# Loading query weights from ScalarE's queue and gate/up weights as 32x32 blocks, with the order of steps made anew

## The chip, the cores and the metric

One core of one Trainium2 chip. The metric is device time of one execution of the kernel, in microseconds (us), and the number compared is the median of several runs. A core has a matrix engine (TensorE, PE in the profile; its weight loads are shown as PEld), VectorE (DVE), ScalarE (ACT), GpSimd (POOL) and SyncE (SP). SP and ACT also issue transfers (DMAs) from memory; in the profile their issues are shown as SPq and ACTq. Each engine runs its own instructions in order; between engines there are semaphores.

## What is computed

For each of 16 batch elements x (256 tokens of 256 channels): attention with 16 heads under a mask, an RMS norm with a gain and a shift made from a condition vector, a time-mixing layer with a linear recurrence, a rotation, and a gated feed-forward layer whose operands are quantized to FP4 in blocks of 16. Cut to its frame (the weights of the first layer are written Wq to Wo, those of the mixing layer ak to ao):

```python
q, k, v = x @ Wq.T, x @ Wk.T, x @ Wv.T              # 16 heads of 16
o = softmax(q @ k.T * 0.25, masked) @ v @ Wo.T
xn = rms_norm(o) * (1 + sc) + shift                  # sc, shift = silu(cond) @ Wc.T + bc
x = x + (sigmoid(r) * wkv_scan(k2, v2)) @ ao.T       # k2, v2, r: xn mixed with its neighbour, @ ak, av, ar
xq = quant(rotate(x))                                # one 256x256 rotation from cond and q_right
h = silu(xq @ quant(w_gate).T) * (xq @ quant(w_up).T)
out = x + quant(h) @ quant(w_down).T
```

w_gate and w_up are 704x256, w_down is 256x704. quant divides each block of 16 by its largest absolute value over 6, rounds to the FP4 grid and multiplies back.

## The kernel before, in words

Each batch element goes through stages, each a Python generator that yields after a few instructions: `ask` (a: load and transpose x, project q, k, v), `attend` (t), `leave` (l: output projection and norm), `mix` (m), `rotate` (r), `hidden` (h, i: gate and up for each half of the tokens), `turn_h` (d, e) and `down` (f). Beside them stand the stages that prepare the weights: `loads` (L), `turn_w` (Q for Wq, Wk, Wv; O for Wo; A for ak, av, ar, ao), `turn_mask` (K), `modulate` (M), `times` (T), `rotation` (R), `in_weights` (W0 to W5) and `out_weights` (V0, V1). The string ORDER at lines 27 to 75 names, token by token, which generator takes its next step; that is the order of the program, and each engine gets its instructions in it. Nothing reorders them later.

Transfers. `loads` (line 209) issues in this order: x of element 0 as four transfers (`load_x`, line 139, on SP: one for each group of 64 channels, in pieces of 64 floats, so that 32x32 blocks lie where VectorE's block transpose wants them), Wq, the 13 small vectors (line 222, on ACT's queue, into the tile `rows`), Wk, the mask, Wv, Wo, Wc, and the four matrices of the mixing layer. All but the vectors are issued by SP. Transfers use eight semaphores in turn: one that takes a semaphore waits until the transfer that had it before has landed, and what is behind it on its queue waits too.

Weights. `turn_w` (line 292) transposes a matrix on PE in four 128x128 pieces into a PSUM bank and copies the bank out (q, k, v, o on DVE, line 305; the others on ACT, line 307). `in_weights(j)` (line 514) loads up to two groups of 128 rows of the concatenated gate and up weights (128x256 each, 1 KB a row), quantizes them as 128x512 (the last block as 128x256), transposes them on PE (line 531) and copies them from PSUM into `guT` on ACT (line 535). There are six such blocks.

`quant` (line 481) is used for weights and activations alike: on DVE the largest absolute value (488), its scaling (490), a reciprocal (491) and a product (492); on ACT an absolute value (494); on DVE two rounding steps (496, 497); on POOL the product back (500). I call lines 488 to 492 the first half and 496 to 497 the second. Its small tiles are double-buffered. x of each element is transposed by DVE in 32x32 blocks (line 605). `turn_mask` makes `keep` from the mask, which the value copies of every element read (line 640). `modulate` makes `sil` on DVE (352 to 354), which a matmul reads (358); `rotation` writes 32 small products on POOL (423, 428) that DVE multiplies by `mgain` (433) before PE combines them (439).

PSUM: four banks serve the scores (`pss`), four everything else (`ps`), taken in turn, so that each use of a `ps` bank waits for the reader of the fourth use before it.

Before all of it stand 12 transposes of the identity into an unused bank (line 183), and POOL's memsets.

Of the kernel before, what the change touches and what calls it, by code (L numbers as in the profile page):

```python
# [17 lines left out]
P = 128  # L18
# [6 lines left out]


ORDER = """
L L L L W1 L Q Q L K L a0 W5 a0 W1 W1 K K Q Q Q W1 Q a0 L W1 a0 R a0 K a0 L W5 R L W0 W1 K K K W5 A R t0 a0 L A
W1 O t0 L a0 W3 R W5 W5 W0 M a1 A O t0 A W5 a1 R M a2 W5 t0 t0 t0 a1 R a1 t0 W0 W3 t0 R W3 W3 t0 W2 a1 t0 t0 a1
M a1 t1 a1 W0 A W3 V0 t1 t1 R R A M t0 W0 W3 a2 R t1 W0 V0 M t1 W2 t1 t0 W3 t1 t1 W4 a3 V1 W0 t0 A t0 M t0 t1 V0  # L30
t0 a3 t0 A T W2 W2 t1 T t1 V0 t1 a2 a2 a2 t1 l0 a2 t1 a2 t1 V0 l0 l0 t1 V0 a2 W4 W2 t1 l0 V0 a4 l0 l0 t2 l0 m0
t1 V1 W4 a3 t2 t2 a3 a3 m0 m0 m0 m0 m0 t2 t2 a3 W4 V1 t2 m0 m0 m0 l1 l1 l1 m0 m0 m0 l1 t2 W4 m0 m0 m0 m0 m0 t2
t2 t2 t2 l1 V0 l1 l1 a3 a3 V0 t2 t2 r0 V1 t2 W4 m1 m1 t2 W2 m1 m1 r0 a4 m1 t3 m1 W4 t3 t2 m1 m1 V1 t2 t3 t3 t2
W2 V1 r0 t3 t3 m1 m1 m1 m1 r0 V1 a4 l2 l2 m1 m1 m1 m1 t3 m1 a4 r0 t3 l2 t3 t3 a4 t3 t3 l2 r1 r1 r0 t3 r0 a4 l2
t3 t3 r1 r1 r1 l2 l2 a4 a4 a5 t3 r0 r0 a5 r0 m2 m2 t4 t4 t3 t3 m2 m2 a6 i0 i0 i0 i0 t4 i0 i0 i0 i0 i0 i0 i0 i0
i0 i0 m2 m2 m2 m2 m2 r1 r1 r1 r1 m2 t4 t4 m2 t4 r1 m2 a5 a5 a5 a5 a5 a5 m2 l3 t5 l3 t4 l3 l3 h0 m2 m2 m2 t4 t5
m2 h0 h0 h0 h0 h0 h0 l3 h0 h0 h0 r2 t5 l3 l3 V1 h0 i1 h0 r2 t4 r2 a6 V1 h0 m3 t4 i1 a7 h0 r2 i1 h1 i1 r2 t4 h1
h1 i1 t4 h1 t4 t4 h1 h1 h1 t4 m3 m3 a6 h1 h1 t5 a6 h1 r2 h1 r2 t4 t5 t4 i1 a6 r2 r2 t5 h1 h1 i1 r2 m3 a6 t5 i1
i1 i1 i1 t5 t5 h1 m3 t5 t4 t5 t5 a6 a6 m3 m3 t6 t6 m3 m3 m3 i1 i1 m3 m3 i2 i2 i2 i2 i2 m3 e0 e0 i2 i2 t6 t6 e0
i2 l4 i2 t6 i1 i2 i2 t6 h2 h2 e0 t5 m3 m3 m3 l4 h2 t6 l4 h2 m3 h2 t6 l4 h2 i2 h2 h2 h2 h2 t5 r3 h2 t5 l4 r3 a7  # L40
d0 l4 t5 h2 t6 t5 t5 l4 i2 m4 d0 d0 m4 a8 h2 t6 d0 h2 i2 a7 r3 t6 a7 a7 t6 t6 t6 t6 a7 m4 m4 m4 r3 r3 a7 a7 m4
m4 m4 t7 l5 t7 t7 l5 m4 m4 m4 m4 m4 t6 t7 l5 l5 l5 r3 m4 m4 e1 m4 m4 l5 l5 t7 t6 t6 f0 f0 f0 f0 r4 t7 r3 r4 a8
r3 e1 e1 e1 r3 f0 t7 t7 t7 d1 d1 r4 t7 t7 d1 r3 r4 i3 a9 d1 r4 i3 m5 m5 i3 i3 i3 i3 i3 a8 r4 m5 m5 i3 i3 i3 t7
a8 a8 a8 i3 i3 i3 m5 m5 t8 m5 m5 m5 l6 l6 a8 a8 l6 r4 h3 h3 l6 t8 t8 m5 h3 h3 h3 f1 m5 m5 t8 t8 i3 l6 t8 h3 f1
m5 m5 h3 h3 t7 r4 r4 r4 f1 l6 m5 m5 l6 h3 h3 h3 m5 t8 t8 t7 t7 t7 t7 t8 r5 t8 f1 t8 i4 i4 m6 t8 t8 r5 a9 d2 h3
h3 i4 d2 i4 aa i4 t8 m6 h3 t8 m6 a9 r5 r5 r5 a9 a9 a9 t8 t9 t7 d2 r5 r5 t8 t9 m6 i4 d2 r5 r5 r5 i4 i4 i4 i4 e2
m6 e2 m6 a9 i4 e2 i4 t8 e2 a9 m6 m6 l7 i4 l7 m6 m6 m6 t9 l7 l7 f2 f2 m6 m6 m6 m6 l7 l7 l7 l8 l8 t9 h4 m7 h4 l8
h4 m6 l8 m6 m7 f2 h4 f2 h4 h4 h4 h4 r6 h4 h4 l8 m7 m7 t9 t9 r6 l8 l8 h4 t9 t9 t9 r6 aa e3 f1 r6 i4 i5 h4 t9 e3
e3 e3 h4 i5 i5 i5 i5 t9 m8 r6 i5 m7 i5 i5 h4 r6 aa m7 i5 aa t9 t9 t9 ab t9 m8 i5 i5 i5 d3 f2 m7 r6 d3 h5 h5 h5
h5 h5 aa aa h5 i5 r6 r6 ta t9 h5 t9 h5 m7 h5 ta ta h5 h5 m7 h5 aa ta r6 h5 m8 aa m7 d3 d3 m7 m7 m7 m7 h5 m7 f3  # L50
m7 m7 f3 f3 f3 m8 m8 ta ta ta m8 ta m8 ta r7 r7 m8 m8 m8 ta ta d4 d4 ta i5 ta ta ta ab f3 i6 i6 i6 i6 i6 i6 i6
i6 i6 i6 i6 h6 h6 h6 h6 h6 h6 h6 h6 h6 h6 i6 ab ab ab ab d4 d4 ta tb h6 m8 h6 t9 m8 e4 e4 i6 h6 ab m8 ta ta e4
m8 ac r7 m8 l9 tb m8 i6 ab e4 f4 f4 l9 r7 h6 r7 f4 l9 l9 l9 m8 e5 tb r8 tb f4 l9 l9 f4 r8 d5 ac m9 m9 m9 r8 e5
r8 r7 r7 tb m9 la d5 r7 la la m9 m9 r8 la ac ac m9 m9 m9 m9 m9 r8 r7 tb m9 d5 m9 r7 ac m9 la d5 la la m9 ac tb
m9 tb tb i7 ma ma tb tb ad i7 i7 i7 i7 i7 i7 i7 i7 e5 e5 i7 i7 i7 tb tc tc tc m9 r8 i7 f5 f5 i7 ma f5 f5 d6 f5
r8 d6 r9 tb h7 r9 tb h7 ad r8 tb ma r8 h7 h7 h7 h7 r9 r9 h7 h7 h7 ma ma tb r9 ma r9 tc tc tc tb h7 h7 h7 ad ad
tb r9 ac ac ma ma ma ma ma h8 h8 h8 tc ma ma d6 h8 h8 d6 tc ad i8 ma ma ad r9 i8 i8 i8 i8 i8 i8 h8 h7 h8 tc i8
i8 i8 h7 ma h8 e6 h8 e6 e6 e6 h8 lb h8 h8 r9 f6 lb i8 i8 r9 f6 h8 f6 f6 ra i8 lb lb lb f6 tc tc ra e7 lb lb e7
tc h8 i8 i9 tc i9 i9 i9 ae tc ra tc mb e7 i9 mb ad ra ra td d7 e7 i9 ad tc ra i9 ae d7 td td mb mb ra tc i9 tc
i9 mb td td h9 ra i9 mb i9 mb td mb h9 mb h9 i9 h9 h9 h9 mb h9 h9 h9 d7 d7 td h9 h9 td td i9 h9 h9 lc lc td lc  # L60
af mb ae ra mb lc f7 mb mb i9 ae lc lc ra mb f7 mb lc mc ia mc h9 ia ia ia ia f7 f7 ia ia ia td ia ia ia ia mb
rb rb td td d8 td ae rb f7 ia td rb ae ae mc d8 te td mc d8 mc ae rb ia d8 rb td e8 mc td mc mc af mc e8 e8 e8
mc mc mc rb mc ld mc mc f8 te mc te te rb rb ld ld ld te ha f8 f8 ha mc ha ha rb te ha f8 ha ha ha te ha ib ha
ha ha te te te te te ib ha rc ib ib ib ib ib ib ld ld ld te rc ha ib rc ib ib e9 hb d9 rc md e9 af te rc md hb
ib hb f8 te hb md hb ib e9 md d9 af te te af e9 hb rc rc ib rc te C md af hb hb hb hb hb d9 d9 tf md af af md rc
rc hb hb le le md md tf f9 tf le md md f9 le md tf md md md md md tf tf ic ic ic ic ic f9 f9 ic ic ic le hb rd
ic le ic tf ic rd le ic me f9 rd tf ic da tf rd rd da ea hc ea hc hc rd ea ic me hc da ea tf hc rd hc tf da me
me me me tf tf hc rd me hc hc tf tf hc hc me me hc me tf tf rd tf hc me fa me me me me fa fa rd db fa me lf id
db lf fa id id id id lf lf id id id me db id id id hc lf C hd hd lf db hd lf id hd hd eb re id eb eb hd hd mf mf
id eb hd re re hd fb re hd dc hd re fb fb mf re dc fb hd mf fb mf mf re hd mf ec ec ec dc dc mf ec re fc hd mf  # L70
fc mf fc mf mf ed re fc dd fc ed mf re dd mf mf mf mf ed ie ed ie ie ie ie ie ie ie dd rf dd ie ie he C he ie he
rf rf ie C rf he ie he ie he rf fd he he he rf rf rf fd he fd he rf ee fd rf if if he he if ee if if he if if if
if hf hf if hf if if hf ee ee fd hf if hf de if hf hf hf de de de hf hf fe hf hf fe hf fe fe ef ef ef fe ef df
df df df ff ff ff ff ff
"""


# [1 line left out]
def kernel(  # L79
# [56 lines left out]
    x_sb = {}  # L136
    queue = [nc.sync]

    def load_x(b):
        if b < B:  # L140
            t = io.tile([P, S // 32, 64], F32, tag="x", name="x_sb", bufs=2)
            for a in range(4):
                queue[0].dma_start(
                    out=t[32 * a : 32 * a + 32], in_=x[b].rearrange("(q i) (a c) -> a i q c", i=32, a=4)[a]
                )
            x_sb[b] = t

    flat = lambda a: a.rearrange("p t e -> p (t e)")
# [31 lines left out]
    make_identity(nc, ident)  # L180

    warm = ps()
    for i in range(12):
        nc.tensor.transpose(warm[:, 0:P], ident, ident)


# [22 lines left out]
    def loads():  # L209
        def load_w(name, src, tag, bufs=1):  # L210
            w_in[name] = lent(tag, bufs)
            if name == "ao":

                nc.sync.dma_start(out=w_in[name], in_=src.rearrange("(p h) c -> p h c", h=2))
            else:
                nc.sync.dma_start(out=w_in[name], in_=src.rearrange("(t p) c -> p t c", p=P))

        load_x(0)
        yield
# [8 lines left out]
        yield  # L228
        load_w("k", w_k, "er")
        yield  # L230
        nc.sync.dma_start(out=mask_u, in_=mask.rearrange("(t p) k -> p t k", p=P))
        yield
        load_w("v", w_v, "kv")
        yield
        load_w("o", w_o, "num")
        yield
# [275 lines left out]
    nc.gpsimd.memset(downT[FF % P : P, FK - 1, :], 0.0)  # L512

    def in_weights(j):
        j *= 2 * P
        nt = min(2, (2 * FF - j) // P)
        n = nt * E
        raw = wk.tile([P, FF], F32, tag="h", name="raw", bufs=2)[:, 0:n]
        for jj in range(nt):
            lo, hi = j + jj * P, j + (jj + 1) * P  # L520
            for src, base in ((w_gate, 0), (w_up, FF)):
                a, b = max(lo, base), min(hi, base + FF)
                if a < b:
                    nc.sync.dma_start(out=raw[a - lo : b - lo, jj * E : (jj + 1) * E], in_=src[a - base : b - base, :])
        yield
        wq = yield from quant(raw, n, "hq", 4)
        pt = ps()
        for ct in range(E2):
            for jj in range(nt):
                at = ct * nt + jj  # L530
                nc.tensor.transpose(
                    pt[:, at * P : (at + 1) * P], half(wq[:, jj * E : (jj + 1) * E], ct), ident
                )
        yield
        nc.scalar.copy(guT[:, :, j : j + nt * P], pt[:, 0 : E2 * nt * P].rearrange("p (t n) -> p t n", t=E2))
        yield

    def turn_half(src, dst, k0):
# [413 lines left out]
        "L": loads, "Q": lambda: turn_w("q", "k", "v"), "K": turn_mask, "O": lambda: turn_w("o"), "M": modulate,  # L952
        "T": times, "A": lambda: turn_w("ak", "av", "ar", "ao"), "R": rotation, "C": check,
    }
    for j in range(6):
        stages[f"W{j}"] = lambda j=j: in_weights(j)
    for j in range(2):
        stages[f"V{j}"] = lambda j=j: out_weights(j)
# [157 lines left out]
```

## Time and profile before

| what | value |
|---|---|
| median of 3 runs (lowest, highest) | 678.1 us (677.49, 678.19) |
| the profiled execution's own time | 678.29 us |
| its span in the profile | 676.4 us |
| DVE busy, ACT busy | 580.9 us, 353.7 us |
| first matmul (identity transposes) | 2.37 us |
| first transposes of Wq, Wk, Wv | 6.92, 8.38, 11.05 us |
| first scores | 18.35 us |
| last matmul ends, near | 671 us |
| time of packets on the main DMA queue, share of 16 engines | 7.6% |
| idle of PE between 11.05 us and 590 us | under 0.2 us |

Reading it: the profile has one row for each group of like instructions, written as line, engine, operation, output tile <- input tiles. "busy" is the time in which an engine worked, "idle before" the time in which it stood still just ahead of a group, with the releaser that ended it. The chain of waits is followed back from the last instruction: at each step to whatever released it. The timeline lists instructions in order of start. One program matmul of fp32 appears as two rows of the hardware, so a projection of four shows as eight; a transpose shows as one.

### The profile page before, as it was taken

The numbers are of one execution on the slowest core, as the hardware profiler recorded it, in microseconds if no ns is written. First come the engines' busy times: TensorE is split into PE (matmuls) and PEld (weight loads), VectorE is DVE, ScalarE is ACT, GpSimd is POOL, SyncE is SP. The second block draws the span as 40 slices with busy tenths as digits, with TensorE's granted clock in tenths as the row PEclk, the third lists the DMA queues.
The fourth block names the chain that finished last, engine by engine and source line by source line (L and its number), as shares of the span: only waits on it lengthen the run. The fifth ranks groups of instructions, "written<-read, shape, count | busy, mean of one in ns | idle before, by whom it ended". The sixth has DMA issues, their size and how long they took to land.

```text
span 676.4 us, 10441 instructions
## 1 busy us (share of the span) xinstructions
PE 662.4 (98%) x3928; PEld 467.7 (69%) x3928; DVE 580.9 (86%) x973; ACT 353.7 (52%) x777; POOL 147.0 (22%) x171
## 2 busy tenths in 40 slices
PE   6999999999999999999999999999999999999995
PEld 5667666756677766866777767676776677768774
DVE  6887988998897868888989898898998898999971
ACT  1788756564574465555344644273454554343232
POOL 4802311311222021130203120130311313031210
PEclk9999999999999999999999999999999999999999
DMA  5520000000001001010010100010000000001001
GB/s 160 131 69 1 9 9 17 1 16 0 1 17 29 5 1 32 1 25 9 5 28 1 32 5 12 1 32 1 16 1 17 1 0 17 1 16 31 10 9 36
DMA packets 37327, 13.63 MB, mean 20 GB/s; under 512 B 32900, under 2 KB 36884, under 8 KB 37268
## 3 DMA queue, kind: packets, MB, share of 16 engines
q1 hardware_dynamic: 37152, 12.85, 7.6%
q8 instruction: 33, 0.54, 0.3%
q14 instruction: 26, 0.21, 0.1%
q10 hardware_dynamic: 116, 0.02, 0.0%
HBM read 8.67 MB, written 4.19 MB: 19 GB/s over the span
## 4 chain that ended last, share of the span: by engine, by line
PE 90%; DVE 6%; DMA 1%; ACT 1%; issue 0%; SPq 0%; POOL 0%; ACTq 0%; POOLq 0%; DVEq 0%
PE ps L567 24%; PE ps L880 21%; PE pss L656 10%; PE ps L934 9%; PE ps L677 9%; PE ps L579 8%; PE ps L543 3%; PE ps L843 2%; PE ps L917 2%; PE ps L591 1%; DVE v L496 1%; DVE v L497 1%; DVE h L897 1%; DVE am L488 1%; PE ps L301 1%; DVE v L492 1%
## 5 line engine op out<-in xcount | busy, mean ns | idle before, releaser
L880 PE MATMUL ps<-guT,xqT 128*128 128x352 f32 x512 | 163.9, 463 | 0.5 <-ACT xqT L865 0.3
L665 ACT ACTIVATE w<-pss 128x512 f32<-128x512 f32 x256 | 133.7, 606 | 41.5 <-PE pss L656 41.3
L880 PEld LDWEIGHTS ps<-guT,xqT 128*128 128x128 f32 x512 | 94.1, 190 | 55.0 <-issue 3.7
L500 POOL TENSOR_TENSOR hq<-v,am 128x704 f32<-128x704 f32 (+2 forms) x40 | 56.0, 1401 | 203.0 <-DVE v L497 147.0
L656 PE MATMUL pss<-qT,kT 32*128 32x512 f32 x512 | 74.0, 640 | 0.0
L934 PE MATMUL ps<-hT,downT 128*128 128x256 f32 x312 | 70.7, 380 | 0.0
L494 ACT ACTIVATE m<-v 128x704 bf16<-128x704 f32 (+2 forms) x56 | 40.7, 729 | 50.1 <-DVE v L492 40.8
L934 PEld LDWEIGHTS ps<-hT,downT 128*128 128x128 f32 x312 | 58.9, 190 | 10.1 <-DVE h L897 0.8
L677 PE MATMUL ps<-w,v_one 128*32 128x256 f32 x1024 | 61.7, 382 | 0.0
L891 ACT ACTIVATE th<-ps 128x352 f32<-128x352 f32 x64 | 30.2, 472 | 56.2 <-PE ps L880 54.3
L814 DVE RECIPROCAL den<-den 128x512 f32<-128x512 f32 x16 | 53.6, 3348 | 0.5
L496 DVE SCALAR_TENSOR_TENSOR v<-m,v 128x704 f32<-128x704 bf16 (+2 forms) x56 | 47.1, 841 | 5.1 <-ACT m L494 5.1
L677 PEld LDWEIGHTS ps<-w,v_one 128*32 128x32 f32 x1024 | 30.1, 109 | 29.4 <-issue 6.3
L497 DVE SCALAR_TENSOR_TENSOR v<-m,v 128x704 f32<-128x704 bf16 (+2 forms) x56 | 47.1, 841 | 1.9
L546 ACT COPY hT<-ps 128x384 f32<-128x384 f32 (+1 forms) x64 | 27.1, 431 | 40.1 <-PE ps L543 40.0
L893 DVE SCALAR_TENSOR_TENSOR th<-th,ps 128x352 f32<-128x352 f32 x64 | 32.4, 506 | 13.3 <-ACT th L891 13.0
L897 DVE SCALAR_TENSOR_TENSOR h<-th,ps 128x352 f32<-128x352 f32 x64 | 33.3, 520 | 8.2 <-PE ps L880 3.9
L500 POOL TENSOR_TENSOR xq<-v,am 128x512 f32<-128x512 f32 x16 | 18.5, 1154 | 87.4 <-DVE v L497 87.4
L543 PEld LDWEIGHTS ps<-ident,hq 128*128 128x128 f32 (+1 forms) x204 | 23.5, 136 | 18.7 <-issue 4.9
L656 PEld LDWEIGHTS pss<-qT,kT 32*128 32x128 f32 x512 | 20.7, 182 | 22.6 <-issue 18.6
L817 POOL TENSOR_TENSOR yT<-num,den 128x512 f32<-128x512 f32 x16 | 20.6, 1288 | 71.1 <-DVE den L814 56.3
L687 DVE STREAM_TRANSPOSE u<-ps 128x512 f32<-128x512 f32 x32 | 22.5, 704 | 14.3 <-PE ps L677 14.3
(175 smaller groups left out, 1191.9 us busy)
## 6 DMA issues: line engine op xcount, KB each, us to landing
x_sb<-in_x_dram SPq DMA_DIRECT2D x64, 64.0 KB, 2.1
out_dram<-o_sb SPq DMA_DIRECT2D x52, 64.0 KB, 1.8
out_dram<-o_sb SPq DMA_DIRECT2D x6, 128.0 KB, 3.9
raw<-in_L_ffn_w_down_dram SPq DMA_DIRECT2D x2, 352.0 KB
raw<-in_L_ffn_w_gate_dram SPq DMA_DIRECT2D x5, 128.0 KB, 3.0
raw<-in_L_ffn_w_up_dram SPq DMA_DIRECT2D x5, 128.0 KB
ek<-in_L_cond_Wq_dram SPq DMA_DIRECT2D x1, 256.0 KB, 3.0
er<-in_L_cond_Wk_dram SPq DMA_DIRECT2D x1, 256.0 KB
```

Source lines behind the costliest of these rows:

```text
L496: nc.vector.scalar_tensor_tensor(v, m, 1.5 * 2.0**22, v, ALU.max, ALU.add)
L497: nc.vector.scalar_tensor_tensor(v, m, 1.5 * 2.0**22, v, ALU.max, ALU.subtract)
L500: nc.gpsimd.tensor_tensor(blk(dst), blk(v), bc(am), ALU.mult)
L543: nc.tensor.transpose(pt[0:n, (k - k0) * P : (k - k0 + 1) * P], src[:, k * P : k * P + n], ident)
L567: nc.tensor.matmul(pool_tile[:, ot * n : (ot + 1) * n], w[:, ct, ot * P : (ot + 1) * P], src[ct], start=(ct == 0), stop=(ct == E2 - 1),)
L579: nc.tensor.matmul(pool_tile[:, tt * E : (tt + 1) * E], srcT[:, ct, tt * P : (tt + 1) * P], w[:, ct, :], start=(ct == 0), stop=(ct == E2 - 1),
L656: nc.tensor.matmul(quad[r], kT[rows_, g, kt * P : (kt + 1) * P], qT[rows_, g].rearrange("p i q -> p (i q)"), start=True, stop=True,)
L665: nc.scalar.activation(w[:, kt, r].rearrange("p i q -> p (i q)"), quad[r], AF.Exp)
L677: nc.tensor.matmul(pu[32 * r : 32 * r + 32, i * S : (i + 1) * S], vo[:, kt, 8 * g + 2 * r + i, :], w[:, kt, r, i, :], start=(kt == 0), sto ...
L814: nc.vector.reciprocal(flat(den), flat(den))
L880: nc.tensor.matmul(p_[:, 0:FH], xqT[:, ct, tt * P : (tt + 1) * P], guT[:, ct, base + f * FH : base + (f + 1) * FH], start=(ct == 0), stop= ...
L934: nc.tensor.matmul(pdn[:, 0:S], downT[:, k, h * P : (h + 1) * P], hT[:, k, :], start=(k == 0), stop=(k == FK - 1))
```

## The change

Five things are changed.

1. Wq is issued from ACT's queue, and in the new order ahead of the small vectors (it stands first there, before the load of the activation table). Wk and Wv stay on SP and follow x of element 0 directly; the mask comes after Wv.
2. The gate and up weights are loaded in four blocks of 352 rows (each half of gate, each half of up), each as four transfers in pieces of 256 bytes, as x is, and quantized as 128x704.
3. They are transposed by DVE in 32x32 blocks, straight into `guT`; the PE transposes and ACT's copies of these weights are gone.
4. The warm-up has 8 transposes instead of 12.
5. ORDER is another string throughout. W4 and W5 no longer exist; W0 to W3 have six steps instead of seven. In the new string, x of element 1 is loaded and `ask` of elements 0 and 1 and `attend` of element 0 begin earlier among the weight steps.

```diff
+    def in_blocks(t, src, engine):
+        for a in range(4):
+            engine.dma_start(out=t[32 * a : 32 * a + 32], in_=src.rearrange("(q i) (a c) -> a i q c", i=32, a=4)[a])
+
     def load_x(b):
         if b < B:
             t = io.tile([P, S // 32, 64], F32, tag="x", name="x_sb", bufs=2)
-            for a in range(4):
-                queue[0].dma_start(
-                    out=t[32 * a : 32 * a + 32], in_=x[b].rearrange("(q i) (a c) -> a i q c", i=32, a=4)[a]
-                )
+            in_blocks(t, x[b], queue[0])
...
-    for i in range(12):
+    for i in range(8):
         nc.tensor.transpose(warm[:, 0:P], ident, ident)
...
-                nc.sync.dma_start(out=w_in[name], in_=src.rearrange("(t p) c -> p t c", p=P))
+                engine = nc.scalar if name == "q" else nc.sync
+                engine.dma_start(out=w_in[name], in_=src.rearrange("(t p) c -> p t c", p=P))
...
         load_w("k", w_k, "er")
         yield
+        load_w("v", w_v, "kv")
+        yield
         nc.sync.dma_start(out=mask_u, in_=mask.rearrange("(t p) k -> p t k", p=P))
-        yield
-        load_w("v", w_v, "kv")
         yield
...
     def in_weights(j):
-        j *= 2 * P
-        nt = min(2, (2 * FF - j) // P)
-        n = nt * E
-        raw = wk.tile([P, FF], F32, tag="h", name="raw", bufs=2)[:, 0:n]
...
-        wq = yield from quant(raw, n, "hq", 4)
-        pt = ps()
-        for ct in range(E2):
-            for jj in range(nt):
-                at = ct * nt + jj
-                nc.tensor.transpose(
-                    pt[:, at * P : (at + 1) * P], half(wq[:, jj * E : (jj + 1) * E], ct), ident
-                )
-        yield
-        nc.scalar.copy(guT[:, :, j : j + nt * P], pt[:, 0 : E2 * nt * P].rearrange("p (t n) -> p t n", t=E2))
+        src = (w_gate, w_up)[j // 2][(j % 2) * FH : (j % 2 + 1) * FH]
+        raw = wk.tile([P, FF], F32, tag="h", name="raw", bufs=2)
+        in_blocks(raw.rearrange("p (q c) -> p q c", c=64), src, nc.sync)
+        yield
+        wq = yield from quant(raw, FF, "hq", 4)
+        nc.vector.transpose(
+            guT[:, :, j * FH : (j + 1) * FH].rearrange("p h (q i) -> p h q i", i=32),
+            by_blocks(wq.rearrange("p (q c) -> p q c", c=64)),
+        )
         yield
```

The new ORDER begins so (a0 and a1 are `ask` of elements 0 and 1, t0 is `attend` of element 0); the old one began `L L L L W1 L Q Q L K L a0 W5 a0 W1 W1 K K Q Q`:

```
L L L L L a0 a0 L Q Q Q W1 L a0 K L Q a1 a0 a0 a1 a0 Q K t0 Q a0 K t0 t0 K W1 K R W0 R W3 K t0 t0 K a1 W1 a0 W1
```

## The prediction

> **What bounds the kernel now.** I read the busy totals first, then the chain of waits in order of time, then the opening in the timeline. The page's first part:
>
> ```profile
> PE 662.4 (98%) x3928; PEld 467.7 (69%) x3928; DVE 580.9 (86%) x973; ACT 353.7 (52%) x777; POOL 147.0 (22%) x171
> ```
>
> TensorE (PE) is busy for 662.4 of 676.4 us; a microsecond of PE work removed, or of PE wait in the opening, is worth about one at the end. VectorE (DVE) is second. The chain says where PE does not yet run back to back:
>
> ```profile
> 3.53 0.24 ACTq L224
> ...
> 4.23 2.84 DMA rows<-in_cond_dram
> ...
> 7.08 0.35 SPq L524
> ...
> 7.47 0.44 SPq L231
> ...
> 7.95 2.96 DMA kv<-in_L_cond_Wv_dram
> ...
> 11.05 1.10 PE ps L301 x4
> 12.14 4.93 PE ps L567 x16
> ...
> 17.51 0.47 PE ps L531 x4
> 18.42 1.07 PE pss L656 x8
> ```
>
> Columns: start, length, what. Until 11.05 the chain is made of transfers: cond's landing releases the gate weights' issue on SP (every transfer waits for an earlier one with which it shares a semaphore), behind it stand the mask's and the value weights' issues, and these land at 10.91. From 11.05 on it is PE, through the first scores at 18.4. In the timeline, PE's own speed changes on the way:
>
> ```profile
> 11.94 3.41 PE L567 MATMUL ps<-xT,wt_q 128*128 128x256 f32 x8
> 15.19 1.89 PE L567 MATMUL ps<-xT,wt_k 128*128 128x256 f32 x8
> ```
>
> The same eight matmuls take 3.4 us (0.43 each) and then 1.9 (0.22 each); the granted clock reads 1.00 in both, so the column does not show it. The stretches of ten microseconds show what stands beside PE:
>
> ```profile
> 10.00:20.00 10.00, 8.95 (x43) 7.06 (x44) 9.00 (x29) 4.34 (x8) 4.27 (x10) 1.00 0.63 167
> 20.00:30.00 10.00, 10.00 (x80) 6.52 (x79) 8.00 (x17) 8.13 (x18) 8.77 (x25) 1.00 0.60 157
> 30.00:40.00 10.00, 10.00 (x66) 7.10 (x65) 9.66 (x19) 8.22 (x18) 3.89 (x3) 1.00 0.14 37
> ```
>
> After the length come PE, PEld, DVE, ACT, POOL, clock, DMA share. DVE stands at 9.0, 8.0 and 9.7 of 10 with PE full: it has little to give here.
>
> **PE work removed.** The 22 transposes of gate and up weights (L531). Eight of them are 0.95 us of the chain at 78.42: 0.119 each, 2.6 in all, on the path. The four dropped warm-up transposes (12 in 2.82 us from 2.37) lie where PE waits for the query weights anyway: nothing.
>
> **DVE.** Six quantizations become four, over the same elements. One of 704 is 0.90+0.20+0.44+0.89 for the first half (2.5 with gaps, as from 650.30) and 0.89+0.89 for the second: 4.2, four are 16.8. Before: 0.69+0.18+0.35+0.69 and 0.68+0.69, 3.3 for each of five blocks, some 2.2 for the short one, 18.7. Added are four 32x32-block transposes of 704:
>
> ```profile
> L605 DVE STREAM_TRANSPOSE xT<-x_sb 128x512 f32<-128x512 f32 x6 | 4.2, 693 | 0.0
> ```
>
> 693 ns for 512, so 0.95 for 704 by length (between 0.7 and 1.3), 3.8 in all. DVE gains 1.9 us of work. ACT loses six evacuations (L535, 0.61 and once 0.41) and two m: some 3.8, no bound there.
>
> **DMA.** Gate and up become 16 issues instead of 12, of 256-byte pieces as x has. From the page:
>
> ```profile
> x_sb<-in_x_dram SPq DMA_DIRECT2D x64, 64.0 KB, 2.1
> raw<-in_L_ffn_w_gate_dram SPq DMA_DIRECT2D x5, 128.0 KB, 3.0
> ```
>
> 88 KB in such pieces I take at 2.1 to 4.1 us (2.9 scaled by bytes); an issue costs SP 0.48 (x4 in 1.94) against 0.41, so 2.8 us more on SP's queue, where x, the mask and later weights stand behind. The share of 0.63 leaves room. The Trainium skill's DMA: Bandwidth & Descriptors, Specifications, says that transfers reach line rate from 512 bytes on and that below it there is a read-modify-write; that speaks against this part. By an estimate from its 435 GB/s, 1.44 MB at half rate would hold all engines 3.3 us longer over the first 30 us. The row of x shows pieces of 256 bytes landing no later, so the sum has nothing for it.
>
> **The opening, walked through the new order.** I take each engine's instructions in the changed program in turn, with durations from the rows.
> - Query weights issue at 0.7 on ACT instead of 3.88; 3.0 to land (3.88 to 6.92), so 3.7 to 4.2. Their transposes end at 5.3. The vectors behind them slip: mix_k now waits for that landing, and the last of the 13 lands near 9.4 (before 8.1); nothing reads them before 11.4.
> - Key weights wait for decay's landing (about 4.0) and land at 7.0; their transposes end at 8.1.
> - wt_q on DVE now stands behind xT (x lands near 5.1) and parq. parq took 2.75 us at 2.87, its end falling with the last of POOL's memsets; now it meets them only at their end: 6.4. wt_q is done by 7.1, so PE is what the query projection waits for: 8.1 to 11.5 at the slow rate, key projection to 13.3, value transposes to 13.8, first scores at 14.1 (kT 0.58).
> - Before, first scores were at 18.35, with mask and a_k transposes (0.44 each) and four L531 (0.47, counted above) already done. The start is worth 18.35 - 14.1 - 0.88 - 0.47 = **2.9**.
>
> The Trainium skill's TensorE: Matmul & The Clock Gate, Part 1, says that the array runs at half clock until a window of some 3.4 us was busy. The row agrees: busy without a break from 11.05, fast from about 15. By the page, an estimate, key transposes at 7.0 would end the slow stretch near 10.5 and take 0.5 off; the sum does without it.
>
> **What is late next.** DVE starts later than PE gains: wt_v at 13.8 (before, quantization began at 9.36), then without pause: wt_v 0.7, mask 0.4, first weights 2.5, keep 0.7, the norms 0.8, v_one 0.6, some/odd 1.0, second half 1.7 (22.2), second weights 2.5, xT and mgain 1.0, third weights 2.5, u 0.7, x1T 0.6 = 29.5. PE, meanwhile: scores, value projection 1.75, mask, scores, query and key projection of element 1 (1.75 each), w_c, values 1.9, scores, value projection, a_k, scores: 28.6. There the third query projection needs the PSUM bank that x1T empties: it waits **0.9**.
> DVE goes on: divide 1.1, two second halves 3.4 (34.0); then the multiply by mgain (L433) waits for POOL, whose 32 rotation products (26 took 9.5 us from 21.71, 0.37 each) stand behind a product that now ends at 23.6: 35.4. Multiply 1.3, u 0.7, wt_o 0.7, two first halves 5.0, sil 1.4 = 44.5. PE reaches the matmul that reads sil at 41.3 and waits **3.2**. Everything behind it in PE's order waits too: rotation, a_o, scores, the first output projection. That is taken over the bounds 0 (before held DVE at 0.8 to 0.97 here and PE never waited over 0.1) and 6 (another 2 if a landing or POOL is later): I stay at 4.1, the walk's own rows.
>
> **Sum.** 2.6 + 2.9 - 4.1 = 1.4 us less. The profiled execution took 678.29 (span 676.4 and 1.9 around it): 676.9. The median of the runs is 678.1, 0.2 below it: **676.7**.
>
> The end of the order I leave at nothing: PE's last wait, 1.16 us for POOL's product at 663.58, stays. In the new order two second halves (1.7 each) stand together at DVE's end: between 0.9 longer and 1.2 shorter.
>
> **Rivals.**
> 1. *The plan holds and PE never waits for DVE* (0.22). For it: before, PE waited for nothing from 11.05 to 599. Against: DVE has 30.7 us of queue between 13.8 and sil. Time: 678.1 - 5.5 = 672.6; with a short wait or two up to 674.
> 2. *DVE becomes the bound up to element 4's transpose* (0.21), slower. Counting the new order's instructions by their rows, 62 us of DVE stand between wt_v and that transpose (30.7 of them up to sil); at full use it is reached at 76, and PE, with the walk's waits, at 80. From 10 to 90 us DVE reached 68.7 of 80, 86%; at that share the 62 take 72, to 86: 6 us more than the sum if the projection behind it follows at once, 3 if PE has other work meanwhile: 679.7 to 682.7. It decides from 4 us of DVE idle in that stretch on. For it: the sum of idle there before was 11 us. Against: part of that idle is DVE waiting for a PE that was itself full.
> 3. *The ends cancel* (0.17): the start's gain is eaten by the waits and a longer tail (0.7): 677.4 to 678.3. That holds also if x, not the weights, limits the start: the fourth piece of x waits for the first (2.7) and may land at 6.
>
> **Chances.** The forecast's own case (0.40) runs from 675.5 to 677.9, half of it on either side of 676.74, which is 0.2% below the median; 0.2% is about what a measurement here can tell from no change. Faster: 0.22 + 0.23 = 0.45. Same: 0.17 + 0.16 = 0.33. Slower: 0.21 and a little, 0.22. The range takes rival 1's shorter half and most of rival 2: 673.0 to 680.6.
>
> **What would show it.** No L531; PE's first value transposes near 13 and first scores at 13.5 to 14.5; the third query projection waiting for DVE x1T; the matmul that reads sil waiting for DVE about 3 us near 42 to 45; DVE over 0.93 from 14 to 50. Wrong would be: first scores past 15.5 (landings later than taken), no PE wait over 0.5 before 60 (rival 1), or PE waits for DVE going on past 50 (rival 2).

## The result and the profile after

The changed kernel takes 682.46 us (median of 5 runs, 680.98 to 684.02) against 678.1 (677.49 to 678.65) for the kernel before: a ratio of 1.0061, 95% interval 1.0046 to 1.0076, so 4.1 us slower by the ratio. I had forecast 676.7 with 673.0 to 680.6 as the range. The time lies outside it, and the sign is wrong. The profiled execution took 682.46 with a span of 680.6, 4.2 more than before.

The first part of its page:

```profile
PE 663.0 (97%) x3902; PEld 467.8 (69%) x3902; DVE 576.0 (85%) x965; ACT 349.6 (51%) x769; POOL 146.5 (22%) x169
```

PE has 26 instructions less (22 transposes and 4 warm-up ones) and is yet busy for 0.6 us **more**. So some of what remained ran slower. PE's rows of the opening in the timeline (start, length, engine and line, operation, count, and in brackets the idle time before it with what ended it):

```profile
7.89 1.12 PE L304 MATMUL ps<-ident,er 128*128 128x128 f32 x4 [2.44 <-DMA er<-in_L_cond_Wk_dram]
8.81 3.33 PE L559 MATMUL ps<-xT,wt_q 128*128 128x256 f32 x8
12.25 1.99 PE L559 MATMUL ps<-xT,wt_k 128*128 128x256 f32 x8
14.92 1.14 PE L648 MATMUL pss<-qT,kT 32*128 32x512 f32 x8 [0.21 <-ACT kT L624]
```

The first scores come at 14.92 instead of 18.35. The same view, around the matmul that reads sil:

```profile
42.84 0.66 PE L304 MATMUL ps<-ident,xq 128*128 128x128 f32 x4
46.27 1.86 PE L361 MATMUL ps<-sil,x1T 64*128 64x16 f32 x8 [2.77 <-DVE sil L357]
48.06 2.07 PE L442 MATMUL ps<-x1T 128*128 128x128 f32 x8
49.93 1.06 PE L304 MATMUL ps<-ident,yT 128*128 128x128 f32 x4
50.91 1.99 PE L648 MATMUL pss<-qT,kT 32*128 32x512 f32 x8
```

The wait of 2.77 is the one forecast (3.2). What follows was not: four transposes take 1.06 (the four at 42.84 took 0.66), eight scores 1.99 (1.14 in the opening). The kernel before has the sil matmul (1.86 above) and the rotation (2.07 above) in the other order, faster and with no wait:

```profile
34.50 1.11 PE L439 MATMUL ps<-x1T 128*128 128x128 f32 x8
...
37.94 1.06 PE L358 MATMUL ps<-sil,x1T 64*128 64x16 f32 x8
```

In the changed kernel the stretches of one microsecond, PE alone, show what goes with it (columns: stretch, length, PE busy, granted clock, DMA share, GB/s):

```profile
45.00:46.00 1.00, 0.00 (x0) 0.93 0.55 217
46.00:47.00 1.00, 0.73 (x4) 0.50 0.00 0
...
52.00:53.00 1.00, 1.00 (x9) 0.66 0.00 0
53.00:54.00 1.00, 1.00 (x5) 1.00 0.23 53
```

From 45.85 to 52.68 the granted clock is 0.50. The kernel before shows 1.00 throughout this part. At the end of the kernel it happens once more, here in the timeline of all engines:

```profile
664.04 0.88 PE L535 MATMUL ps<-ident,hq 128*128 128x128 f32 x6 [0.58 <-POOL hq L503]
...
666.32 0.87 PE L535 MATMUL ps<-ident,hq 128*128 128x128 f32 x6 [1.40 <-POOL hq L503]
...
667.49 1.22 PE L909 MATMUL ps<-downT,hT 128*128 128x256 f32 x2 [0.29 <-ACT hT L538]
...
669.36 3.32 PE L909 MATMUL ps<-downT,hT 128*128 128x256 f32 x12
```

The same place in the kernel before:

```profile
663.58 0.87 PE L543 MATMUL ps<-ident,hq 128*128 128x128 f32 x6 [1.16 <-POOL hq L500]
664.74 0.70 PE L917 MATMUL ps<-downT,hT 128*128 128x256 f32 x2 [0.29 <-ACT hT L546]
...
665.72 2.76 PE L917 MATMUL ps<-downT,hT 128*128 128x256 f32 x12
```

Two matmuls that took 0.70 before take 1.22, twelve that took 2.76 take 3.32. In the changed kernel the clock is 0.50 from 667.08 to 670.49.

Where the 4.2 us of span come from, by the two traces:

| item | us | how read |
|---|---|---|
| 22 transposes less on PE | -2.6 | 0.119 each |
| start | -2.1 | 18.35 - 14.92 - 0.88 - 0.47 |
| PE waits from 30 to 46.3 | +3.5 | 0.39 + 0.33 + 2.77 |
| half clock behind the wait | +3.0 | 0.80 + 0.96 + 0.40 + 0.85, the sil matmul, the rotation, four transposes and eight scores against the same at 1.00 |
| wait for ACT's rnorm near 593 | +1.1 | not there before |
| tail, from the end of the last gate and up product | +2.5 | 18.64 (657.06 to 675.70) against 16.15 |
| together | +5.4 | measured 4.2; 0.4 of the rest is a wait for x1T that only the kernel before has, 0.8 I did not trace |

### The profile page after: what moved, and what is told of

It reads as the page before. It is cut to its first block, busy times and chain, and to the rows that moved or that the text cites. A ratio compares the mean times of both kernels' runs of the same rounds, so it can differ in the third digit from the quotient of the medians.

```text
span 680.6 us, 10380 instructions
## 1 busy us (share of the span) xinstructions
PE 663.0 (97%) x3902; PEld 467.8 (69%) x3902; DVE 576.0 (85%) x965; ACT 349.6 (51%) x769; POOL 146.5 (22%) x169
## 4 chain that ended last, share of the span: by engine, by line
PE 92%; POOL 3%; DVE 2%; DMA 1%; ACT 1%; issue 0%; ACTq 0%; POOLq 0%; DVEq 0%
PE ps L559 24%; PE ps L872 23%; PE ps L926 10%; PE pss L648 9%; PE ps L571 8%; PE ps L669 8%; PE ps L535 3%; PE ps L835 2%; PE ps L909 2%; PE ps L583 1%; POOL x1T L426 1%; POOL x1T L431 1%; POOL hq L503 1%; DVE v L500 1%; DMA er<-in_L_cond_Wk_dram 0%
## 5 line engine op out<-in xcount | busy, mean ns | idle before, releaser
L503 POOL TENSOR_TENSOR hq<-v,am 128x704 f32<-128x704 f32 x38 | 55.4, 1458 | 160.4 <-DVE v L500 126.0
L497 ACT ACTIVATE m<-v 128x704 bf16<-128x704 f32 (+1 forms) x54 | 40.3, 747 | 47.6 <-DVE v L495 47.5
L500 DVE SCALAR_TENSOR_TENSOR v<-m,v 128x704 f32<-128x704 bf16 (+1 forms) x54 | 47.1, 872 | 1.9
L499 DVE SCALAR_TENSOR_TENSOR v<-m,v 128x704 f32<-128x704 bf16 (+1 forms) x54 | 45.1, 835 | 3.1 <-ACT m L497 2.7
L885 DVE SCALAR_TENSOR_TENSOR th<-th,ps 128x352 f32<-128x352 f32 x64 | 32.4, 506 | 16.5 <-ACT th L883 16.1
L535 PE MATMUL ps<-ident,hq 128*128 128x128 f32 (+1 forms) x204 | 32.3, 277 | 2.0 <-POOL hq L503 2.0
```

The costliest lines, as they stand in the source:

```text
L499: nc.vector.scalar_tensor_tensor(v, m, 1.5 * 2.0**22, v, ALU.max, ALU.add)
L500: nc.vector.scalar_tensor_tensor(v, m, 1.5 * 2.0**22, v, ALU.max, ALU.subtract)
L503: nc.gpsimd.tensor_tensor(blk(dst), blk(v), bc(am), ALU.mult)
L535: nc.tensor.transpose(pt[0:n, (k - k0) * P : (k - k0 + 1) * P], src[:, k * P : k * P + n], ident)
```

## The experiments

My theory after this: **a wait of PE costs its own length and then a stretch at half clock; the time was lost where VectorE stands in an unlucky order, in the opening and in the tail.** (The tail is the time from the end of the last gate and up product.) Rivals: the slow stretches have another cause; VectorE has too much work, whatever the order; the block transposes or the moved loads cost by themselves. Differences below are the ratio to the kernel before less 1, times 678.

| kernel | median us | ratio (95% interval) | to before, us |
|---|---|---|---|
| changed | 682.46 | 1.0061 (1.0046 to 1.0076) | +4.1 |
| fill_sil | 678.77 | 1.0009 (0.9996 to 1.0021) | +0.6 |
| sil_early | 679.24 | 1.0016 (1.0005 to 1.0027) | +1.1 |
| open_order | 680.18 | 1.0037 (1.0020 to 1.0054) | +2.5 |
| open_late | 679.02 | 1.0019 (1.0008 to 1.0029) | +1.3 |
| tail_order | 680.66 | 1.0044 (1.0028 to 1.0059) | +3.0 |
| warm_start | 680.25 | 1.0030 (1.0017 to 1.0042) | +2.0 |
| all_four | 676.07 | 0.9971 (0.9961 to 0.9981) | -2.0 |
| late_start | 682.29 | 1.0063 (1.0050 to 1.0076) | +4.3 |
| start_alone | 677.93 | 0.9997 (0.9989 to 1.0006) | -0.2 |
| blocks_alone | 684.72 | 1.0104 (1.0088 to 1.0120) | +7.1 |
| blocks_warm | 686.01 | 1.0119 (1.0103 to 1.0135) | +8.1 |
| before_warm | 676.67 | 0.9982 (0.9973 to 0.9991) | -1.2 |

### fill_sil: the wait stays, PE does not stand idle

```
         pm = ps()
+        for _ in range(23):
+            nc.tensor.transpose(pm[:, 0:P], ident, ident)
         for t in range(4):
```

> The changed kernel with 23 identity transposes more on PE, written into the bank of the sil matmul just ahead of it, where PE waits 2.77 us for sil. They need no data, take 2.7 us at 0.119 each, and nobody reads them. Clock theory: the matmuls behind the wait ran at a granted clock of 0.50 (45.85 to 52.68) because PE stood idle; kept busy, they run at 1.00, the wait itself stays, and the kernel takes the 3.0 us less that the slow matmuls cost: 679.5. Rival, the slow stretch has another cause (the chip's load, the kind of work, the moment): 682.5 as before, the slow stretch is still there. Should the transposes come late: 683.5 or more.

Measured 678.77, 3.5 us less than the changed kernel by the ratios. PE's timeline there:

```profile
44.27 2.67 PE L361 MATMUL ps<-ident 128*128 128x128 f32 x23
47.11 1.06 PE L363 MATMUL ps<-sil,x1T 64*128 64x16 f32 x8 [0.16 <-DVE sil L357]
48.10 1.21 PE L444 MATMUL ps<-x1T 128*128 128x128 f32 x8
49.16 0.60 PE L304 MATMUL ps<-ident,yT 128*128 128x128 f32 x4
```

The sil matmul still starts only when sil is there (2.84 us after the useful work before it ended). But 23 transposes that nobody reads keep PE busy, and the groups behind run at 1.06, 1.21, 0.60 instead of 1.86, 2.07, 1.06. The clock theory holds for this stretch; a slow stretch of another cause would have stayed. The mean granted clock that is recorded with every execution agrees: 0.990 to 0.995 in the five of the changed kernel, 0.995 to 0.999 in the twelve of fill_sil.

### sil_early: one token, the wait alone

Token M.4 (the fourth M in ORDER; the number counts the tokens of one stage) makes sil on VectorE. It moved from behind the fifth quantization's first half to ahead of the multiply by mgain.

> The changed kernel with one token moved: VectorE's three small sil instructions (0.57 us), which PE waits 2.77 us for, stand ahead of the multiply by mgain, where VectorE stood idle for 3.24 us. The wait at the sil matmul goes. Theory (VectorE as a whole is late there): the wait moves to the output projection (it needs the divide, which ends at 50.1, and PE is there at 47.5): 2.6 us of the same length three matmul groups later, and the same chance of a half-clock stretch behind it: 681.5 to 682.5. Rival (the one step was misplaced): 5.8 us less, 676.7.

Measured 679.24: between the two, 3.0 less than the changed kernel. The wait at the sil matmul is gone, but it came back in **pieces**:

```profile
41.48 1.93 PE L669 MATMUL ps<-w,v_one 128*32 128x256 f32 x32 [1.57 <-DVE u L679]
...
48.07 2.58 PE L648 MATMUL pss<-qT,kT 32*128 32x512 f32 x8
```

1.57 stand ahead of the values, where the changed kernel has 0.33. The 1.24 more match the 1.23 by which the multiply by mgain, ahead of that u on VectorE, took longer in this profile (1.72 for 0.49). The trace does not show why it did, so this piece is not shown to come from VectorE's order or load. The eight scores stretch from 1.14 to 2.58: their weight loads in the profile each wait some 0.2 us for ScalarE's exponentials, which are late and empty the banks one by one. That is 3.0 in all. The clock stays at 1.00 from 30 to 60. So nearly the whole gain is the half-clock stretch that did not come. My expectation had taken the wait to move in one piece.

### open_order and open_late: VectorE's order, then its load

In the changed kernel VectorE stands still for POOL, with the quantizations behind:

```profile
38.65 0.49 DVE L436 TENSOR_SCALAR x1T<-x1T,mgain 128x512 f32<-128x512 f32 x1 [3.24 <-POOL x1T L431]
38.70 3.03 POOL L503 TENSOR_TENSOR hq<-v,am 128x704 f32<-128x704 f32 x2
```

open_order moves W3.5 and W0.5 (POOL's products) ahead of R.7, and M.4 and R.8 behind V0.2, with t0.18 (divide) ahead of it (R.7 and t0.18 leave places outside the lines shown; the numbers behind the points are added here, the kernel has none):

```
-t0.16 W0.4 t1.2 O.1 R.8 t0.17 A.3 O.2 W0.5 t1.3 V0.2 t1.4 a2.4 W3.5 W2.2 V1.1 t1.5 M.4 t1.6
+W3.5 t0.16 W0.4 t1.2 O.1 t0.17 A.3 O.2 W0.5 R.7 t1.3 t0.18 V0.2 t1.4 a2.4 M.4 R.8 W2.2 V1.1 t1.5 t1.6
```

> The changed kernel with five tokens moved in the opening, no work added or taken: on POOL the two products of the quantizations stand ahead of the last 8 rotation products; on VectorE the multiply by mgain (which waited 3.24 us for those products) and sil stand behind the first half of the next quantization, and the first divide ahead of it. Theory (VectorE is late because its order makes it stand still for POOL, not because it has too much work): PE no longer waits at the sil matmul (2.77), nor at the values (0.33), and the half clock behind it (3.0) does not come: 6.1 less, 676.4; up to 677.9 if a new wait of 1 to 1.5 us appears at the down weights' transposes behind it. Rival (VectorE has too much work before element 4, whatever the order): the wait moves to the next matmul that needs VectorE, 2 us or more with a slow stretch of its own: 681 to 682.5.

Measured 680.18. PE no longer waits at the sil matmul and the clock stays at 1.00 through the opening, but VectorE at 9.8 and 9.6 of 10 from 30 to 50 gives a wait of 1.09 at the next u and scores of 2.58 again. It is 1.6 less than the changed kernel, against 6.1 expected at best.

open_late has the same moves, and V0.2 to V0.9 and V1.2 to V1.7 (the down weights, first read at 192 us) some 40 to 120 tokens later.

> The changed kernel with the five moves of open_order, and besides the quantization of the two blocks of the down weights (first read at 192 us) moved out of the opening: their VectorE, ScalarE, POOL and PE steps stand some 10 to 60 us later. No work is added or taken. open_order still waited 1.1 us for VectorE u and PE's scores stretched from 1.14 to 2.58 us there, with VectorE at 9.6 to 9.8 of 10 from 30 to 50. Theory (VectorE was given too much too early; the work itself is not too much): no PE wait over 0.5 us between 16 and 190, 2.5 us less than open_order: 677.7. Rival (VectorE has too much work before the first hidden products, wherever it stands): PE waits appear between 50 and 130 instead, and the time stays at 680 or above.

Measured 679.02, 1.3 above the theory's number. The waits over 0.5 us between 16 and 190 are gone (0.4 and 0.4 are left), so the work itself is not too much; it was due too early. The stretched scores (2.58) are still there: an idle time that the profile books as a busy PE, and that I had not counted.

### tail_order: the last second half

Token if.13 moved from behind hf.11 to ahead of hf.9, as it stood before.

> The changed kernel with one token moved at the end: the second half of the quantization of the last element's first hidden chunk stands ahead of the second chunk's two gate products on VectorE again (as in the kernel before) instead of behind the front half of the last quantization. If the longer end (18.6 us from the last L872 against 16.1 before) comes from these two second halves standing together: the last transposes start some 0.9 us earlier, the wait of 0.58 goes, PE's idle time in that stretch falls from 2.3 to some 1.4 us and with it the clock of 0.50 from 667.1 to 670.5, worth 1.7 us: 679.9. If the slow clock there is not tied to the idle time: 681.6. If the end is longer for another reason: 682.5.

```profile
663.90 0.87 PE L535 MATMUL ps<-ident,hq 128*128 128x128 f32 x6 [1.47 <-POOL hq L503]
665.07 0.70 PE L909 MATMUL ps<-downT,hT 128*128 128x256 f32 x2 [0.30 <-ACT hT L538]
```

In the profile the tail takes 16.5 us (16.15 before, 18.64 in the changed kernel), with 0.70 for the two matmuls that took 1.22: the clock stays at 1.00 to the last product. By the times it is 680.66, only 1.1 less than the changed kernel with about 1 us of uncertainty on either. The direction is confirmed; the full 2.2 is seen in one execution only. In eight of the nine profiles that keep the changed tail the clock falls there, after 1.70 to 1.99 us of idle time in one stretch of the clock's grid (see below); in the ninth, clock_probe2, 1.76 did not lower it. In the two that mend the tail (this one, 1.47, and all_four, 1.55) it does not fall.

### warm_start and late_start: what the start is worth

```
             pt = ps()
+            for _ in range(11 if name == "k" else 0):
+                nc.tensor.transpose(pt[:, 0:P], ident, ident)
             for ct in range(E2):
```

> The changed kernel with 11 identity transposes more on PE ahead of the key weights' transposes, where PE waits 2.44 us for the weights to land, at the cold rate 0.235 each, 2.6 us. Clock theory: the query projection runs slow (3.33 us for what takes 1.89) because PE was idle from 5.46 to 7.89; filled, it runs fast and the first scores come 1.2 to 1.5 us earlier. In the end that is worth nothing or little here, since PE waits for VectorE later: the wait at sil takes up what the start gains, 681.0 to 682.5. If the slow first projection had nothing to do with idle time: first scores at 14.9 or later, 682.5 to 683.

```profile
5.33 2.54 PE L300 MATMUL ps<-ident 128*128 128x128 f32 x11
...
8.50 1.89 PE L561 MATMUL ps<-xT,wt_q 128*128 128x256 f32 x8
...
13.17 1.14 PE L650 MATMUL pss<-qT,kT 32*128 32x512 f32 x8 [0.21 <-ACT kT L626]
```

The first projection takes 1.89 for 3.33 and the first scores come 1.75 earlier: here the clock theory is right. My statement on the end was wrong: the time fell by 2.1 us. The wait at sil is still 2.8, and the sil matmul starts 1.71 earlier (44.56 for 46.27): VectorE's chain up to sil begins with copies of what PE has turned, so it moves with the start and does not take up the gain. In this profile the half clock behind that wait lasted 3.41 us, not 6.83, so the 2.1 need not be the start's alone.

late_start puts the query weights back on SP (`engine = nc.sync`), behind x.

> The changed kernel with the query weights back on SP's queue, behind x; the rest of the change stays. If the early query weights are worth what the prediction said of the start (2.9 us for the whole new start, most of it theirs): 2 to 3 us slower, 684.5 to 685.5, unless VectorE's lateness swallows it: PE's first matmuls come later, VectorE's chain up to sil is bound by POOL, and then the wait at sil shrinks by as much: 682 to 683. Rival (key weights, not query weights, end the start): no difference, first scores still near 14.9.

```profile
6.66 1.13 PE L304 MATMUL ps<-ident,ek 128*128 128x128 f32 x4 [2.32 <-DMA ek<-in_L_cond_Wq_dram]
8.01 1.13 PE L304 MATMUL ps<-ident,er 128*128 128x128 f32 x4 [0.21 <-DMA er<-in_L_cond_Wk_dram]
```

Measured 682.29, ratio 1.0063 against 1.0061, first scores at 14.91. The rival holds: query weights 2.3 us later cost nothing, since the key weights land at 7.9 to 8.0 either way.

### all_four: the mended version

open_late with the edits of tail_order and warm_start.

> open_late with the one token of tail_order and the 11 transposes of warm_start. The parts stand at different places (start, opening, end), so their gains should add: open_late's 677.7 less 1.8 less 2.2, 673.7; that would be faster than the kernel before by 0.6%. If the warm start only sharpens a wait for VectorE in the opening: 675.5 to 676.

Measured 676.07: 0.29% faster than the kernel before (interval 0.19 to 0.39%) and 6.1 us less than the changed kernel. The parts add to 6.0 (2.8 + 1.1 + 2.1). It misses the 673.7 I expected by the amounts that open_late and tail_order had missed. In its profile PE waits for nothing over 0.5 us from 2.4 to 587.

### The two parts of the change alone, and the old kernel warmed

start_alone is the kernel before with the new list of loads in the old order.

> The kernel before, with the other part of the change alone: the new list of loads (query weights on ScalarE's queue, key and value weights ahead of the mask) in the old order. The first raw piece of the gate weights still stands ahead of the value weights, and the key weights' place moves by one vector load only. Theory from late_start (the queue of the query weights is worth nothing by itself, the landing of the last weights ends the start): value weights land 0.5 us earlier at most, mask transposes 0.5 later: 677.5 to 678.2, not to be told from no change. By the prediction's walk, in which the early query weights bring the query transposes to 5.3: up to 1.5 less, 676.5.

Measured 677.93, no difference; in its profile the first scores come at 19.12, no earlier than the 18.35 before. So the gain of the start in the changed kernel is one of the order, not of the list. I take it to be the gate weights' first piece, which now stands behind the value weights; no run moves that alone.

blocks_alone is the kernel before with `in_weights` of the change and the old order (W2 and W4 and the PE steps left out, W5 driving the third piece).

> The kernel before, with one part of the change: gate and up weights in four pieces turned on VectorE as 32x32 blocks, and the old order of everything else (the tokens of four of the six old blocks drive the four new ones, those of the two others and the old PE steps fall out). Query, key, value weights and the vectors are loaded as before. If the block part is worth its PE work (22 transposes, 2.6 us) and VectorE carries it in the old order: 675.5. The two issues more of the first piece stand ahead of the mask and the value weights on SP, up to 0.9 us later there: 676.4. If VectorE's extra transposes and longer pieces make PE wait even in the old order, as the prediction's second rival has it: 678 or more. The prediction's share of this part was 2.6 less, and it put the waits down to the start being early.

Measured 684.72, far above the 675.5 and 676.4 of the expectation's first two cases; only the third, 678 or more, has room for it:

```profile
28.54 0.69 DVE L595 STREAM_TRANSPOSE xT<-x_sb 128x512 f32<-128x512 f32 x1
...
29.38 3.40 PE L557 MATMUL ps<-xT,wt_q 128*128 128x256 f32 x8 [4.11 <-DVE xT L595]
```

With 704 elements a piece instead of 512, the pieces at the old places fill VectorE (9.6 and 9.7 of 10 from 10 to 30) and the second element's transpose stands behind them: 4.11 us of wait and again half clock, from 28.9 to 32.3. Dropping the two late tokens also put the four pieces all early, so this prices the pieces **in that order**, not the pieces as such.

blocks_warm adds 7 and 6 warm-up transposes.

> blocks_alone with 7 identity transposes more ahead of the query weights' transposes and 6 ahead of the value weights', where PE waits for landings (1.73 and 1.54 us). By warm_start (2.2 us less for a first projection at full clock): the first projection takes 1.9 instead of 3.4 us, 1.5 less than blocks_alone: 674 to 675, faster than the kernel before by 0.5%. If in the old order PE's first projection waits for VectorE's copy of the query weights or x anyway: as blocks_alone.

Measured 686.01. The wait for xT is still 3.7, so an earlier start only meets it sooner, and in its profile the clock falls at 10.8 already: the six transposes ran at full speed, took 0.82 us and were over while PE still waited 2.04 us for the value weights. A fill that is too short loses the clock it was to keep.

before_warm is the kernel before with 8 and 11 such transposes.

> The kernel before with 8 identity transposes more ahead of the query weights' transposes and 11 ahead of the value weights', where PE waits for landings (1.73 and 1.54 us); nothing of the change. It tells how much of what the combined version has won belongs to the change. If the cold first projection (3.41 us for 1.9) is a cost of the kernel before as well: 1.5 less, 676.6, and of the combined version's 676.1 the change with its order mended would have only some 0.5. If the fill gives nothing in the old order (the transposes end too late, or too early for the clock): 678, and the combined version's 2 us belong to the change with its order mended.

Measured 676.67, 1.2 less than before (interval 0.6 to 1.8), first projection 1.89. The intervals of all_four and before_warm overlap, and the two fill different places: what the change itself is worth with its order mended is some 0.75 us by the ratios, and not shown to be more than nothing. The mended order without the fill was not run.

### clock_probe and clock_probe2: the clock by itself

```
+        for n in (2, 5, 3, 7, 4, 6, 8, 1) * 4:
+            pt = ps()
+            for _ in range(16):
+                nc.tensor.matmul(pt, ident, flat(ew_row), start=True, stop=True)
+            nc.vector.tensor_copy(da, pt[:, 0:S])
+            for _ in range(n):
+                nc.vector.tensor_copy(db, da)
+                nc.vector.tensor_copy(da, db)
+            pt = ps()
+            nc.tensor.transpose(pt[:, 0:P], da[:, 0:P], ident)
```

> The changed kernel and behind its last product a measurement of the clock by itself: 32 bursts of 16 matmuls (identity against 512 columns, some 14 us each at full speed), and after each a chain of 2 to 16 copies on VectorE that PE waits for, so that PE stands idle for 0.9 to 4.7 us. Clock theory: the granted clock falls to 0.50 only at moments that lie a multiple of 3.413 us apart, and only when PE was idle for more than a certain part of the 3.413 us before (between 31% and 52% by the stretches seen so far); it comes back at such a moment too, 3.4 or 6.8 us later. Gaps over 3.4 us fall always, those under 1.0 never, those between by where they lie. Rival (a gap must be longer than 3.4 us in one piece, wherever it lies): only the gaps over 3.4 us fall. The time itself is some 520 us longer and means nothing.

All 29 changes of the clock from 660 us on lie on one grid of 3.4133 us, to 0.02 (I call one step of it a stretch). Of the 32 waits, the 12 of 4.5 us and more lowered it, and of the four of 3.89 only the one that put 3.35 into one stretch of the grid; the other three lay 1.95 to either side of a boundary and cost no clock. Up to 2.02 in one stretch never lowered it within the bursts. So the first sentence of the expectation holds, and its threshold does not: I had put it between 31% and 52%, about 1.1 to 1.8 us.

> The changed kernel and behind its last product the measurement of the clock again, with bursts of 96 identity transposes of 128x128 (some 11 us at full speed) instead of 512-column matmuls, and shorter waits between (1.3 to 3.2 us). In the first measurement 2.02 us idle in one 3.413 us stretch did not lower the clock; in the changed kernel's tail 1.77 us did, between transposes. If transposes count for less than dense matmuls: the clock falls after waits that put 1.3 to 2.0 us into one stretch. If they count alike: it falls only where more than 2.0 us lie in one stretch. If transposes alone never hold the clock up: it is 0.50 throughout, and the warm-up transposes at the start are worth nothing.

With transposes around the wait, one fall in clock_probe2's timeline:

```profile
738.08 0.30 PE L976 MATMUL ps<-ident,num 128*128 128x128 f32 x1 [1.92 <-DVE num L974]
```

and the two stretches of the grid around it (columns as above, PE alone):

```profile
735.48:738.89 3.41, 1.49 (x15) 1.00 0.00 0
738.89:742.31 3.42, 3.42 (x19) 0.50 0.00 0
```

Of 1.92 us in one stretch three of five lowered the clock, of 2.03 to 2.42 all seven, of 1.67 and less none inside the bursts. The mark is near half the stretch, and between transposes a shorter wait suffices than between dense matmuls (2.02 without a fall). The tails fit in, with a blurred edge: 1.77 lowered the clock in the changed kernel and 1.70 in two others, while 1.76 did not in clock_probe2's own tail. Between 1.70 and 1.92 us both happen.

## Why the prediction was wrong, step by step

- **"PE work removed ... 2.6 in all, on the path"**: right; the transposes are gone and nothing replaced them on PE.
- **"The start is worth ... 2.9"**: measured 2.1. Mis-sized by the key weights: "land at 7.0", they landed at 7.9, because decay's landing, for which their issue waits, came at 4.96 and not at "about 4.0". The step that gave the query weights a part in it ("their transposes end at 5.3", measured 5.46) described the trace rightly and was worth nothing, by late_start.
- **"waits 0.9" and "waits 3.2"**: measured 0.39 and 2.77, and 0.33 at one more place. The first stood where forecast, at the third query projection, but ended with VectorE's u, not with x1T. Of the second the place, the cause and the size were right, the size by luck: two errors of the walk cancelled. POOL's products ended at 38.6, not 35.4, and PE came to the matmul at 43.5, not 41.3. Part of the first is a misread row: the products that took 9.5 us from 21.71 in the kernel before are 24, not 26, so 0.40 each and not 0.37 (0.9 us over 32); in the changed kernel they took 0.44.
- **"I stay at 4.1, the walk's own rows"**: this is the step that failed. It priced a wait at its own length. Behind the long one PE ran at half clock for 6.8 us, which cost 3.0 more, shown by fill_sil. I had the clock's behaviour in hand for the start and did not apply it to the waits that I forecast. The Trainium skill's TensorE: Matmul & The Clock Gate, Part 1, gives the half clock to one idle window of about 3.4 us, and a wait of 2.77 would pass by that. The runs show that less suffices: 2.36 of 3.41 us idle in the changed kernel's stretch from 42.44 to 45.85, and 1.92 of 3.41 in three of five cases in clock_probe2.
- **"The end of the order I leave at nothing ... between 0.9 longer and 1.2 shorter"**: measured 2.5 longer. The waits account for 0.8 of it (0.58 + 1.40 against 1.16), inside my bound; the half clock behind them for most of the rest, outside it. That is read from the profiles; by the times tail_order shows 1.1 with about 1 of uncertainty.
- **ACT at the last elements**: a wait of 1.1 for rnorm that no step of mine had. It stays in every version with the changed order, and no run tests it.
- **"DVE gains 1.9 us of work"**: meant as 1.9 us more to do; VectorE's busy time fell by 4.9. 2.6 of it is parq (0.17 for 2.75, as the walk had it); the block transposes took 0.88 each (0.95 taken). The remainder I did not trace, and what it was worth no run tests. The sign "DVE over 0.93 from 14 to 50" failed too: 0.85 (30.49 of 36), with 3.24 us of it spent waiting for POOL.
- **"the sum has nothing for it" (256-byte pieces)**: the 88 KB pieces landed in 2.2 us, at the low end of the 2.1 to 4.1 taken. No row shows a cost.
- **Rival 2**, "DVE becomes the bound", gave 679.7 to 682.7 and the sign, but by PE waits going on past 50. They did not (none over 0.35 from 50 to 590), so that the measured 682.46 stands within its numbers is luck.
- **Together**: the start (0.8 short), the half clock in the opening (3.0), the tail (2.5) and rnorm (1.1), less 0.6 for waits that were shorter than 4.1, make 6.8 between forecast and trace; the spans differ from the forecast by 5.6, and the 1.2 between them are those at the foot of the table.

## What to carry to other kernels

Price a wait of the matrix engine with what comes behind it: between transposes a wait of some 1.7 to 1.9 us or more within one of the clock's stretches cost up to 3.4 us again (between matmuls of 512 columns 2.02 did not lower the clock and 3.35 did), so one long wait can be worse than the same time in pieces, and a few matmuls that nobody reads take the sting out of a wait that can't be removed. When work is moved to a second engine, look at the order of that engine's queue first: here nearly the same instructions took 7.1 us more, 4.1 more or 2.0 less than the kernel before, by where they stood and what kept the clock up. A transfer that came earlier was worth nothing here, while the next one ended the same wait.

## What the runs showed of the hardware

- In these profiles the granted clock changes only on a grid of 3.4133 us (29 of 29 changes in clock_probe, 21 of 21 within the span in clock_probe2). The grid does not start with the program: taken modulo 3.413 the changes lie at 1.5 us in the changed kernel, 1.4 before, 0.6 in open_late, 2.4 in tail_order. With the cold start not filled, the first scores come at 14.57 to 15.80 in the profiles of the changed order, and at 13.14 to 13.17 with it filled. How much of the 3 us over which executions of the changed kernel spread is due to that, no run shows.
- The clock comes back after 3.41 us or after 6.83. With up to 0.55 us of idle time in the first half-clock stretch it mostly came back after 3.41 (0.50 in blocks_alone, 0.54 in clock_probe, 0.55 in clock_probe2), with 0.71 to 1.40 only after 6.83 (blocks_warm, clock_probe). The stretches that hold most of the small sil matmuls stand apart: back after 6.83 with 0.42 idle in the changed kernel and with none in clock_probe. Why, no run isolates.
- The granted clock reads 1.00 in the cold start of most profiles although the same matmuls take 3.33 and 1.99 us; only tail_order, start_alone and blocks_warm show 0.50 there. The durations tell it, the column does not.
- parq took 2.75 us beside POOL's memsets and 0.17 behind them. The multiply by mgain took 0.49 in the changed kernel and 1.72 in sil_early, though POOL's product began 0.05 us after its start in both; that difference stays open.
